# Two small users of PSUM get one bank between them, in quarters, and the other tiles turn through three banks instead of four

## The chip, the cores and the metric

The kernel runs on one core of a Trainium2 chip. The metric is device time in microseconds (us), from one launch. A core has engines that each work through a queue of their own in order: TensorE (PE) for matmuls, VectorE (DVE), ScalarE (ACT), GpSimd (POOL) and SyncE (SP), which here only issues DMAs. PE writes its results into PSUM, which has eight banks of 512 fp32 columns on 128 partitions; DVE and ACT read them there. All data in this kernel are fp32 except masks and an identity.

## The reference

Two blocks stand one after the other, over a residual stream of 2 sequences of 2048 tokens with 128 features. Each block is: modulated layer norm, an attention layer, a gated residual, modulated layer norm, a stack of local attention layers, a gated residual. The first stack has 6 layers with 16 heads and windows of 32 tokens; the second has 2 layers with 8 heads and windows of 64. The change lies in these stacks. One layer of a stack, cut to what matters:

```
def attn_layer(x, Wqkv, qs, ksc, Wo):
    q, k, v = split(x @ Wqkv)                  # heads of 64
    q = l2norm(q) * qs ; k = l2norm(k) * ksc   # a root per token and head
    q, k = rotary(q, k)
    out = local_attention(q, k, v)             # own window and the one before
    return out @ Wo
x = attn_layer(shift_tokens(x)) + x
x = ffn_layer(shift_tokens(x)) + x
```

## The kernel before, in words

`l0_attention` computes the first block's attention (about the first 560 us). `local_models` then does both stacks, and between them the second block's linear attention (`linear`, in pieces called by `lstep`). The stream is held transposed, features on partitions, in `hs[0]` (input of a layer's attention) and `hs[1]` (after its attention).

A layer's attention is done in tiles of 128 tokens. There are 8 layers of 32 tiles, 256 tiles in all, tile number `i`. A loop at the end of `local_models` runs one round per tile, and in a round several tiles are in work at different stages: the projection of tile i+3 (i+4 in the second stack), the transposes and scores of the tiles i+2 and i+1, the mixing and output projection of tile i. The steps that the prediction speaks of, with the PSUM tiles that they use:

- `project` (L862): two matmuls into a wide tile of two banks, `ps_qk` (L871), 16 heads of 64. In the first stack a tile needs two of these, called the first and the second unit here; in the second stack one. ACT squares the wide tile into `sq` (L873). DVE multiplies it by the rotary tables into `r` (L883) and `t` (L888), which POOL adds (L894). The tile `t` has a single buffer. After the last unit, DVE sums the squares of each head (L899, once per unit) and computes the inverse root in eight short instructions on 32 columns (`rsqrt_quick`, L167 to L180; the last one writes `rq_y`). These are called the root chain here. POOL then multiplies `r` by `rq_y` (L906). The sums and three scratch operands of the chain stand in PSUM: they are written into the last unit's `ps_qk`, over the columns already used up.
- `turn` (L925): transposes of `r` (`ps_turn`, L938), copied out by ACT.
- `values` (L945): `ps_v` (L957), copied out by ACT, then moved by DMAs.
- `scores` (L976): a wide tile `ps_s`, with a mask (L988) and 64 small products (L997); DVE takes the maximum (L1005, `mx`) and subtracts it (L1007, `sm`). ACT exponentiates (L1014), DVE sums (L1021) and POOL normalizes (L1023).
- `keys_first_`: transposes `ps_pT` (L1032), copied out by ACT.
- `mix`: 64 small products into `ps_o` (L1050), copied out by ACT (L1056).
- `project_out` (L1059): eight matmuls into 128 columns of a tile `ps_y` (L1067); two DVE instructions add them to `hs` (L1073). Called the output projection here.
- `feed_forward`: after every fourth tile of a sequence, seven pieces (`ps_c`, `ps_r`, `ps_f`, `ps_fy`) that are spread over the following rounds, at most two to a round.

PSUM is given out by two pools. `psA` has two wide buffers (two banks each), which `ps_qk` and `ps_s` take in turn. `psT` has four single banks, which all other tiles, `ps_y` among them, take in turn (`bank(name)`).

The program text gives the instructions in the order of the loop. When the program is built, a scheduler sets the order of each engine's queue in `local_models` and adds the waits; on the chip that order is fixed. Two instructions on different engines that touch the same PSUM tile in one bank, one of them writing, are put one after the other by a wait.

Of the kernel before, what the change touches and what calls it, by code (L numbers as in the profile page):

```python
# [11 lines left out]
F32 = mybir.dt.float32  # L12
# [60 lines left out]
def tile_kernel(ctx: ExitStack, tc: tile.TileContext, a: dict, out: bass.AP):  # L73
    nc = tc.nc
    DRAM = bass.MemoryType.DRAM
    PSUM = bass.MemoryType.PSUM
# [24 lines left out]
    def bc(ap, shape):  # L101
        return ap.to_broadcast(list(shape))
# [59 lines left out]
    def rsqrt_quick(scr, n, pool):  # L162

        x, xm, h, p = scr
        nc.vector.tensor_scalar(xm, x, 1e-24, None, ALU.max)  # L167
        y = pool.tile([128, n], F32, name="rq_g")
        nc.vector.tensor_scalar(
            y.bitcast(I32), xm.bitcast(I32), -0.5, RSQ_SEED, ALU.mult, ALU.add  # L170
        )
        nc.vector.tensor_tensor(p, xm, y, ALU.mult)
        hs_ = pool.tile([128, n], F32, name="rq_h")
        nc.vector.tensor_tensor(hs_, p, y, ALU.mult)
        nc.vector.tensor_tensor(h, p, y, ALU.mult)
        nc.vector.scalar_tensor_tensor(p, h, RSQ_A[0], hs_, ALU.add, ALU.mult)
        for c in RSQ_A[1:3]:
            nc.vector.scalar_tensor_tensor(p, p, c, hs_, ALU.add, ALU.mult)
        r = pool.tile([128, n], F32, name="rq_y", bufs=2)
        nc.vector.scalar_tensor_tensor(r, p, RSQ_A[3], y, ALU.add, ALU.mult)  # L180
        return r
# [526 lines left out]
    def local_models(mA, mB, hs0):  # L708
# [3 lines left out]
        wk = ctx2.enter_context(tc.tile_pool(name="f_k", bufs=1))  # L712
        lw = ctx2.enter_context(tc.tile_pool(name="l_w", bufs=1))
        psA = ctx2.enter_context(tc.tile_pool(name="f_psA", bufs=2, space=PSUM))
        psT = ctx2.enter_context(tc.tile_pool(name="f_psT", bufs=4, space=PSUM))

        def wide(name):

            return psA.tile([128, 1024], F32, tag="A", name=f"ps_{name}")

        def bank(name):
            return psT.tile([128, 512], F32, tag="T", name=f"ps_{name}")


        hs = [hs0, states.tile([128, B, N + 1], F32, tag="hs1", name="hs1")]
# [53 lines left out]
        wts = {}  # L779
# [82 lines left out]
        def project(i, u):  # L862
            g, b, t = tiles[i]
            m, _ = layers[g]
            H, units = m.H, m.units
            tb = tabs[g, t]
            hw = hs[0][:, b, t * 128:(t + 1) * 128]
            pq = wide("qk")
            for j in range(2):
                js = slice(512 * j, 512 * j + 512)  # L870
                nc.tensor.matmul(pq[:, js], lhsT=hw, rhs=wts[g, u][:, js], start=True, stop=True)  # L871
            sq = wk.tile([128, 1024], F32, name="sq", bufs=2)
            nc.scalar.activation(sq, pq, AF.Square)  # L873
            r = wk.tile(
                [128, 1024], F32, tag=f"r{u if len(units) == 2 else i % 2}", name="r", bufs=2
            )
            t2 = wk.tile([128, 1024], F32, name="t2", bufs=1)
            same = units[u][0][0] == units[u][1][0]
            for e in range(1) if same else range(2):
                s = units[u][e][0]  # L880
                hn = 16 if same else 8
                es = slice(512 * e, 512 * e + 64 * hn)
                nc.vector.tensor_tensor(  # L883
                    r[:, es].rearrange("p (h d) -> p h d", d=DH),
                    pq[:, es].rearrange("p (h d) -> p h d", d=DH),
                    bc(tb[:, 0, s].unsqueeze(1), (128, hn, DH)), ALU.mult,
                )
                nc.vector.tensor_tensor(  # L888
                    t2[:, es].rearrange("p (h s d) -> p h s d", s=2, d=32),
                    pq[:, es].rearrange("p (h s d) -> p h s d", s=2, d=32)[:, :, ::-1, :],  # L890
                    bc(tb[:, 1, s].rearrange("p (s d) -> p s d", s=2).unsqueeze(1),
                       (128, hn, 2, 32)), ALU.mult,
                )
            nc.gpsimd.tensor_tensor(r, r, t2, ALU.add)  # L894
            st[i]["r", u], st[i]["sq", u] = r, sq
            if u == len(units) - 1:

                for v in range(len(units)):
                    nc.vector.tensor_reduce(  # L899
                        pq[:, 16 * v:16 * v + 16],  # L900
                        st[i].pop(("sq", v)).rearrange("p (h d) -> p h d", d=DH), AX.X, ALU.add,
                    )
                y = rsqrt_quick([pq[:, k * 32:k * 32 + 2 * H] for k in range(4)], 2 * H, wk)
                for v in range(len(units)):
                    rv = st[i]["r", v].rearrange("p (h d) -> p h d", d=DH)
                    nc.gpsimd.tensor_tensor(  # L906
                        rv, rv, bc(y[:, 16 * v:16 * v + 16].unsqueeze(2), (128, 16, DH)), ALU.mult
                    )
# [150 lines left out]
        def project_out(i):  # L1059
            g, b, t = tiles[i]  # L1060
            m, _ = layers[g]
            NO = m.NO
            oT = st[i].pop("o")
            py = bank("y")
            for c in range(4):
                for s in range(NO):
                    nc.tensor.matmul(  # L1067
                        py[:, 0:128], lhsT=wts[g, "o"][:, c * NO + s, :], rhs=oT[:, s, c, :],
                        start=(c + s == 0), stop=(c == 3 and s == NO - 1),
                    )  # L1070
            for lo, sh in ((0, 0), (64, 1)):
                cs = slice(t * 128 + sh, t * 128 + sh + 128)
                nc.vector.tensor_tensor(  # L1073
                    hs[1][lo:lo + 64, b, cs], py[lo:lo + 64, 0:128], hs[0][lo:lo + 64, b, cs],
                    ALU.add,
                )

# [389 lines left out]
        for i in range(-3, n):  # L1467
# [5 lines left out]
            for j in rounds.get(i, ()):  # L1473
                g, b, t = tiles[j]
                jj = j % per
                nu = len(layers[g][0].units)
                more = g < last
                if g == second and t % 4 == 0:
                    while (b, t // 4) not in ready:
                        lstep()  # L1480
                if nu == 2:
                    project(j, 0)
                if more and jj == 4:
                    load_proj(g + 1, 0)
                if more and jj == 6 and g + 1 == second:
                    models[1].consts()
                if jj == 6 and g == second - 1:
                    linear_consts()
                if more and jj == 8:
                    factors(g + 1)  # L1490
                    if 2 == 2:
                        load_out(g + 1)
                if more and jj == 18:
                    load_ff(g + 1)
                if more and jj == 22:
                    fold_ff(g + 1)
                if nu == 2 and more and jj == per - 1:
                    load_proj(g + 1, 1)
# [6 lines left out]
            for j in rounds.get(i, ()):  # L1505
                g, b, t = tiles[j]
                jj = j % per
                nu = len(layers[g][0].units)
                more = g < last
                project(j, nu - 1)  # L1510
                if nu == 2 and more and jj == per - 1 and g + 1 < second:
                    load_proj(g + 1, 2)
                if nu == 1 and more and jj == per - 1:
                    load_proj(g + 1, 1)
                if b == B - 1 and j + 1 < n:
                    tables(*tiles[j + 1][::2])
# [12 lines left out]
            if i >= 0:  # L1529
                g, b, t = tiles[i]  # L1530
                project_out(i)
                if 2 == 1 and i % per == per - 1 and g < last:
                    load_out(g + 1)
                if t % 4 == 3:
                    feed_forward(g, b, t // 4)
# [9 lines left out]
    with ExitStack() as ctx2:  # L1545
        local_models(m0, m1, hs0)
# [63 lines left out]
```

## Time and profile before

| what | value |
|---|---|
| median of 3 runs | 4936.85 us (4933.53 to 4939.53) |
| the profiled execution's own time | 4928.13 us |
| its span, first to last instruction | 4926.3 us |
| PE busy | 4493.8 us, 91% of the span |
| DVE busy | 3949.1 us, 80% |
| ACT busy | 2637.9 us, 54% |
| POOL busy | 2781.2 us, 56% |
| granted TensorE clock, mean | 0.961 |

Busy means that the engine was executing an instruction; PE's is an upper bound, since matmuls are pipelined. The profile's waits name, for each idle stretch of an engine, the instruction that came after it and the one that ended it. The chain is the work followed back from the last instruction. The profile is of one execution, which took 8.7 us less than the median of the runs.

### The profile page before, as it was taken

The numbers are of one execution on the slowest core, as the hardware profiler recorded it, in microseconds if no ns is written. First come the engines' busy times: TensorE is split into PE (matmuls) and PEld (weight loads), VectorE is DVE, ScalarE is ACT, GpSimd is POOL, SyncE is SP. The second block draws the span as 40 slices with busy tenths as digits, with TensorE's granted clock in tenths as the row PEclk, the third lists the DMA queues.
The fourth block names the chain that finished last, engine by engine and source line by source line (L and its number), as shares of the span: only waits on it lengthen the run. The fifth ranks groups of instructions, "written<-read, shape, count | busy, mean of one in ns | idle before, by whom it ended". The sixth has DMA issues, their size and how long they took to land.

```text
span 4926.3 us, 166334 instructions
## 1 busy us (share of the span) xinstructions
PE 4493.8 (91%) x73028; PEld 3066.5 (62%) x73058; DVE 3949.1 (80%) x6840; ACT 2637.9 (54%) x4207; POOL 2781.2 (56%) x1666
## 2 busy tenths in 40 slices
PE   5667799999999999999999999999999998899997
PEld 4445566666666666666666666666666665556554
DVE  6994488888888888888887888888877777788886
ACT  3223355555555555555555555555555555465554
POOL 3332366666666666666666666666655544455552
PEclk8778899999999999999999999999999999999999
DMA  2000222222222322223222322222212111111121
GB/s 78 1 1 25 85 65 67 69 73 70 69 65 64 87 68 65 66 73 76 68 64 64 79 72 65 66 74 69 68 51 59 50 51 46 37 46 49 51 58 41
DMA packets 222468, 295.31 MB, mean 60 GB/s; under 512 B 75657, under 2 KB 95409, under 8 KB 221745
## 3 DMA queue, kind: packets, MB, share of 16 engines
q1 hardware_dynamic: 221744, 284.67, 22.4%
q8 instruction: 576, 9.44, 0.8%
q14 instruction: 148, 1.20, 0.1%
HBM read 40.98 MB, written 10.75 MB: 10 GB/s over the span
## 4 chain that ended last, share of the span: by engine, by line
PE 49%; DVE 25%; ACT 7%; POOL 5%; issue 3%; DMA 0%; SPq 0%; POOLq 0%; DVEq 0%; ACTq 0%
PE ps_qk L871 12%; PE ps_o L1050 5%; PE ps_v L957 5%; DVE ps_qk L899 5%; PE ps_f L1150 5%; DVE t L888 5%; PE ps_turn L938 4%; PE ps_y L1067 4%; POOL r L894 4%; PE ps_s L997 3%; DVE r L883 3%; PE ps_fy L1175 3%; ACT sq L873 2%; DVE rs L1021 2%; PE ps_pT L1032 2%
## 5 line engine op out<-in xcount | busy, mean ns | idle before, releaser
L894 POOL TENSOR_TENSOR r<-r,t 128x1024 f32<-128x1024 f32 x448 | 1060.2, 2367 | 911.8 <-DVE t L888 794.3
L906 POOL TENSOR_TENSOR r<-r,rq_y 128x1024 f32<-128x1024 f32 x448 | 843.8, 1902 | 517.9 <-DVE rq_y L180 495.8
L873 ACT ACTIVATE sq<-ps_qk 128x1024 f32<-128x1024 f32 x448 | 460.6, 1028 | 1082.3 <-PE ps_qk L871 1014.7
L871 PE MATMUL ps_qk<-wp,hs 128*128 128x512 f32 x1792 | 893.8, 621 | 105.7 <-DVE rq_y L180 77.1
L883 DVE TENSOR_TENSOR r<-ps_qk,tb 128x1024 f32<-128x1024 f32 (+1 forms) x512 | 550.7, 1076 | 211.8 <-ACT sq L873 198.4
L1050 PEld LDWEIGHTS ps_o<-pT,v 64*64 64x64 f32 (+1 forms) x26624 | 479.4, 136 | 304.5 <-ACT pT L1033 160.9
L888 DVE TENSOR_TENSOR t<-ps_qk,tb 128x1024 f32<-128x1024 f32 (+1 forms) x512 | 554.1, 1082 | 143.1 <-POOL r L894 142.4
L1023 POOL TENSOR_TENSOR sm<-sm,rs 128x1024 f32<-128x1024 f32 x256 | 487.5, 1904 | 210.2 <-DVE rs L1022 126.9
L1050 PE MATMUL ps_o<-pT,v 64*64 64x32 f32 (+1 forms) x26624 | 531.2, 221 | 37.0 <-ACT pT L1033 19.2
L899 DVE TENSOR_REDUCE ps_qk<-sq 128x16 f32<-128x1024 f32 x448 | 549.0, 1226 | 11.9
L871 PEld LDWEIGHTS ps_qk<-wp,hs 128*128 128x128 f32 x1792 | 310.1, 193 | 364.3 <-issue 236.1
L938 PEld LDWEIGHTS ps_turn<-ident,r 128*128 128x128 f32 x3584 | 411.7, 143 | 125.2 <-issue 99.4
L957 PE MATMUL ps_v<-wp,hs 128*128 128x512 f32 x896 | 481.9, 639 | 1.0 <-ACT oT L1056 0.8
L1067 PEld LDWEIGHTS ps_y<-oT,wo 128*128 128x128 f32 x3584 | 430.2, 193 | 46.9 <-issue 42.5
L938 PE MATMUL ps_turn<-ident,r 128*128 128x128 f32 x3584 | 447.3, 277 | 9.7 <-POOL r L906 4.1
L1067 PE MATMUL ps_y<-oT,wo 128*128 128x128 f32 x3584 | 446.3, 276 | 1.5 <-ACT oT L1056 1.5
L1056 ACT COPY oT<-ps_o 128x512 f32<-128x512 f32 x448 | 244.0, 588 | 281.9 <-PE ps_o L1050 281.2
L1005 DVE TENSOR_REDUCE mx<-ps_s 128x16 f32<-128x1024 f32 (+1 forms) x256 | 312.5, 1221 | 97.4 <-PE ps_s L997 95.6
L997 PE MATMUL ps_s<-kT,qT 64*32 64x64 f32 (+1 forms) x26624 | 377.9, 230 | 0.7 <-issue 0.5
L997 PEld LDWEIGHTS ps_s<-kT,qT 64*32 64x32 f32 (+1 forms) x26624 | 325.8, 107 | 63.7 <-issue 53.0
L1150 PE MATMUL ps_f<-fx,w 128*128 128x512 f32 (+1 forms) x768 | 356.1, 600 | 2.5 <-DVE fx L1133 1.7
L1021 DVE TENSOR_REDUCE rs<-sm 128x16 f32<-128x1024 f32 (+1 forms) x256 | 310.5, 1213 | 51.1 <-ACT sm L1014 49.0
(265 smaller groups left out, 6850.5 us busy)
## 6 DMA issues: line engine op xcount, KB each, us to landing
v<-vn SPq DMA_DIRECT2D x1276, 128.0 KB
v<-vn SPq DMA_DIRECT2D x744, 64.0 KB
v<-vn SPq DMA_DIRECT2D x64, 256.0 KB
wp<-in_L_ffn_Wqkv SPq DMA_DIRECT2D x20, 512.0 KB
xD<-xb SPq DMA_DIRECT2D x24, 256.0 KB
xb<-xD SPq DMA_DIRECT2D x24, 256.0 KB
cs<-in_cos SPq DMA_DIRECT2D x128, 32.0 KB
cs<-in_sin SPq DMA_DIRECT2D x128, 32.0 KB
```

The lines of the kernel that those rows point to most:

```text
L871: nc.tensor.matmul(pq[:, js], lhsT=hw, rhs=wts[g, u][:, js], start=True, stop=True)
L883: nc.vector.tensor_tensor(r[:, es].rearrange("p (h d) -> p h d", d=DH), pq[:, es].rearrange("p (h d) -> p h d", d=DH), bc(tb[:, 0, s].unsq ...
L888: nc.vector.tensor_tensor(t2[:, es].rearrange("p (h s d) -> p h s d", s=2, d=32), pq[:, es].rearrange("p (h s d) -> p h s d", s=2, d=32)[: ...
L894: nc.gpsimd.tensor_tensor(r, r, t2, ALU.add)
L899: nc.vector.tensor_reduce(pq[:, 16 * v:16 * v + 16], st[i].pop(("sq", v)).rearrange("p (h d) -> p h d", d=DH), AX.X, ALU.add,)
L906: nc.gpsimd.tensor_tensor(rv, rv, bc(y[:, 16 * v:16 * v + 16].unsqueeze(2), (128, 16, DH)), ALU.mult)
L938: nc.tensor.transpose(p[:, c * 128:(c + 1) * 128], r[:, cs], ident)
L957: nc.tensor.matmul(p, lhsT=hw, rhs=wv, start=True, stop=True)
L997: nc.tensor.matmul(sp[W * w:W * w + W, c0:c0 + 2 * W], lhsT=qT[64 * q:64 * q + 64, cc, W * w:W * w + W], rhs=kT[64 * q:64 * q + 64, cc, W ...
L1050: nc.tensor.matmul(po[s][64 * q:64 * q + 64, 128 * c + W * w:128 * c + W * w + W], lhsT=v2[kp, w, co:co + 64], rhs=pT[kp, q, c, W * w:W * ...
L1067: nc.tensor.matmul(py[:, 0:128], lhsT=wts[g, "o"][:, c * NO + s, :], rhs=oT[:, s, c, :], start=(c + s == 0), stop=(c == 3 and s == NO - 1),)
L1150: nc.tensor.matmul(ps_[c][0:sz], lhsT=wts[g, "w1"][:, o:o + sz], rhs=S["x"], start=True, stop=True,)
```

## The change

`psT` gets three banks in place of four. The eighth bank becomes one tile, `ps_quarter`, of four quarters of 128 columns. Quarters 0 and 1 hold the root chain's sums and scratch operands for even and odd tiles, which no longer stand in `ps_qk`. Quarters 2 and 3 take the output projection of even and odd tiles, which no longer takes a bank in turn. The arithmetic is the same, and so are the numbers of instructions.

```diff
-        psT = ctx2.enter_context(tc.tile_pool(name="f_psT", bufs=4, space=PSUM))
+        psT = ctx2.enter_context(tc.tile_pool(name="f_psT", bufs=3, space=PSUM))
+        psQ = ctx2.enter_context(tc.tile_pool(name="f_psQ", bufs=1, space=PSUM))
+        quarters = psQ.tile([128, 4, 128], F32, name="ps_quarter")
+
+        def quarter(kind, i):
+
+            return quarters[:, 2 * kind + i % 2, :]
...
+                ss = quarter(0, i)
                 for v in range(len(units)):
                     nc.vector.tensor_reduce(
-                        pq[:, 16 * v:16 * v + 16],
+                        ss[:, 16 * v:16 * v + 16],
...
-                y = rsqrt_quick([pq[:, k * 32:k * 32 + 2 * H] for k in range(4)], 2 * H, wk)
+                y = rsqrt_quick([ss[:, k * 32:k * 32 + 2 * H] for k in range(4)], 2 * H, wk)
...
-            py = bank("y")
+            py = quarter(1, i)
             for c in range(4):
                 for s in range(NO):
                     nc.tensor.matmul(
-                        py[:, 0:128], lhsT=wts[g, "o"][:, c * NO + s, :], rhs=oT[:, s, c, :],
+                        py, lhsT=wts[g, "o"][:, c * NO + s, :], rhs=oT[:, s, c, :],
...
-                    hs[1][lo:lo + 64, b, cs], py[lo:lo + 64, 0:128], hs[0][lo:lo + 64, b, cs],
+                    hs[1][lo:lo + 64, b, cs], py[lo:lo + 64, :], hs[0][lo:lo + 64, b, cs],
```

## The prediction, made before the changed kernel ran

> **What bounds the kernel now.** I read the page first (shares of the engines, chain), then the windows, PE's waits, and the timeline of one round of the first stack.
>
> ```profile
> PE 4493.8 (91%) x73028; PEld 3066.5 (62%) x73058; DVE 3949.1 (80%) x6840; ACT 2637.9 (54%) x4207; POOL 2781.2 (56%) x1666
> PE 49%; DVE 25%; ACT 7%; POOL 5%; issue 3%; DMA 0%; SPq 0%; POOLq 0%; DVEq 0%; ACTq 0%
> 2000.00:3000.00 1000.00, 966.86 (x18456) 665.36 (x18455) 835.12 (x1350) 572.71 (x900) 642.88 (x375) 0.99 0.28 70
> PE ps_qk L871 <- DVE rq_y L180: 77.1, 79, 3.6
> PE ps_qk L871 <- DVE sm L1007: 16.6, 27, 2.3
> ```
>
> In the window the columns are busy us of PE, PEld, DVE, ACT and POOL, then granted clock, DMA share and GB/s. In the first stack PE is busy 97% of the time and DVE 84%: PE sets the pace with DVE close behind. PE's largest wait in the stacks is the one that the change is about: the first `ps_qk` of a round writes the wide buffer in which the root chain of the round before stood, and waits for the chain's last instruction (77.1 us in 79 waits; with the parts put down to other chain instructions about 88).
>
> One plain round (tile 105, no feed-forward piece on PE), from the timeline; columns are start, duration, instruction, idle time before it and what ended that:
>
> ```profile
> 2356.32 1.98 PE L871 MATMUL ps_qk<-wp,hs 128*128 128x512 f32 x4
> 2358.34 1.03 ACT L873 ACTIVATE sq<-ps_qk 128x1024 f32<-128x1024 f32 x1 [6.68 <-PE ps_qk L871]
> 2359.40 1.22 DVE L883 TENSOR_TENSOR r<-ps_qk,tb 128x1024 f32<-128x1024 f32 x1 [0.49 <-ACT sq L873]
> ...
> 2365.42 1.23 DVE L888 TENSOR_TENSOR t<-ps_qk,tb 128x1024 f32<-128x1024 f32 x1 [1.30 <-POOL r L894]
> ...
> 2366.68 2.49 DVE L899 TENSOR_REDUCE ps_qk<-sq 128x16 f32<-128x1024 f32 x2
> ...
> 2366.93 1.95 PE L1067 MATMUL ps_y<-oT,wo 128*128 128x128 f32 x16
> ...
> 2370.34 0.27 DVE L1073 TENSOR_TENSOR hs<-ps_y,hs 64x128 f32<-64x128 f32 x1
> ...
> 2371.31 0.19 DVE L180 SCALAR_TENSOR_TENSOR rq_y<-ps_qk,rq_g 128x32 f32<-128x32 f32 x1
> ...
> 2371.55 1.98 PE L871 MATMUL ps_qk<-wp,hs 128*128 128x512 f32 x4 [0.75 <-DVE rq_y L180]
> ```
>
> The reader is to see two things. From `r` (2359.40) to the end of the chain (2371.50) DVE has one stretch of 12.10 us with hardly a hole, and `ps_qk` waits only 0.75 us at its end. And the output projection `ps_y` starts at 2366.93, 4.57 us before the chain is over: the two have nothing to do with each other.
>
> **Part 1, what is taken away.** `ps_qk` no longer waits for the chain: at most the 88 us above. The chain's instructions stay the same in number and kind (PSUM before and after), so they cost the same. The first unit's sum (L899, 1.23 us) need not follow the second unit's products any more, but in the order of the built program it still does in most rounds (about seven in ten of those of the first stack), and where DVE has no hole it would gain nothing by moving.
>
> **Part 2, what is added.** Chain and output projection now share a bank. In the order of the changed program as built, the first matmul of an output projection carries a wait for DVE, at the count that the chain's last instruction (L180) raises, in 249 of the 256 rounds; the first `ps_qk` carries none. The output projection is ahead of `ps_qk` in PE's queue, so the wait has moved forward, not gone. Queued behind it on PE are the rest of the scores, both `ps_qk` pairs and the transposes of `ps_pT`; DVE waits for them with `hs`, `mx` and `r`, ACT with `sq`. The scheduler answers by putting part of the scores ahead of `ps_y`: in 84 of the 192 rounds of the first stack 30 or more of the 64 products, in the others none or few (with feed-forward matmuls ahead in most).
>
> The plain round then becomes a loop through both engines. From the chain's end: 0.05 to PE's start (2371.50 to 2371.55), `ps_y` 1.88 (start to the start of the scores, 2366.93 to 2368.81), 15 products left of 64 at 1.48/64 each 0.35, then from `ps_qk` to `r` 3.08 (2356.32 to 2359.40), then DVE's stretch 12.10 less 0.5 for the two `hs` instructions, which now come after `ps_y`: 11.6. Sum 16.96 us against 15.23 before (2356.32 to 2371.55). PE's own work there is 15.23 - 0.75 = 14.5, so PE would stand idle 2.5 us a round. What is late next is the whole of DVE's stretch; DVE in turn idles near 2 us while `ps_y` runs.
>
> The same sum for a group of eight rounds (tiles 104 to 111, which hold two feed-forwards), each time the larger of that loop and of PE's own path between two output projections. Tile 104: PE, 18.85. 105: all scores after `ps_y`, loop 18.3. 106: stretch 13.65 in the trace, loop 18.4. 107: stretch 12.57, loop 17.5. 108: DVE's three `u` (L1167, 0.75 each) go behind the chain in the new order, PE bounds, 19.05. 109: first sum early, 1.2 less, 17.2. 110: 18.0. 111: 16.9. Together 144.2. Before, from one `ps_qk` to the next, the eight took 18.84, 15.23, 16.79, 17.10, 19.58, 17.27, 15.23 and 16.75: 136.8. So +7.4. For tiles 96 to 103 the same working gives 143.0 against 134.3: +8.7. The first stack has 24 such groups: +178 to +209. I take 178, since some rounds (weights being folded) are longer already and give less.
>
> [...] The row: before, `ps_y` ran with the chain from 2366.93 on, in different banks. [...] No run before shows two engines in one bank at once.
>
> **Part 3, three banks.** Without `ps_y` the ring serves fewer tiles, with one bank less. By the timeline each now waits for the copy three uses back: the second `ps_v` for the first `oT`, the transposes for `vn`. These copies take 0.54 to 0.59 us and end before or just at the time when PE comes. Bounds: 0, and one copy of 0.59 in each of 256 rounds, 150 us. Where PE waits at `ps_y` anyway it is covered; I take 0. The feed-forward's `ps_f` takes all three banks, but the transposes behind it now come after `ps_y`, in which time `u` empties them.
>
> **Part 4, second stack** (about 3946 to 4850, 64 rounds of 12.6 to 15.3 us). PE is idle 1.1 us a round there for many reasons, and the chain's waits are about 0.1 of it. One unit, half the output projection, and the new order puts `ps_y` behind other matmuls. Bounds: the old waits vanish, -7; or 1.0 a round as in the first stack, +64. I take +15, nearer the low end, since DVE and PE have more holes there. POOL's and SP's instructions are the same in number; copies of `v` by DMA shift with the rest and end no wait of PE in the rows above. The first 560 us are unchanged.
>
> **Sum.** 178 + 0 + 15 = +193 on the profiled execution's own 4928.13: 5121. The median of the runs lies 8.7 above that execution: 5130.
>
> **Rivals.**
> - *The wait at `ps_y` is short* (20 in 100). In PE-heavy rounds the chain ends 8.0 us after the last `ps_qk` ends (2020.08 to 2028.07 in another part of the timeline), as DVE is then not backed up; PE needs 7.1 us to reach `ps_y` (`ps_o` 2.0, `ps_v` 1.9, `ps_turn` 1.75, part of the scores 1.5). If DVE's stretch closes up like that in plain rounds, 0.9 is lost there in place of 0.75, up to 1.8 where `ps_r` or `fve` lie in it: 2 to 4 us a group, +50 to +95, 4987 to 5030. Against it: the stretch of 12.10 has a single hole of 1.30, which POOL's add sets.
> - *Faster* (8 in 100). The chain is over before PE comes to `ps_y`; 88 us go and nothing comes: 4849. It decides where the loop falls below PE's 14.5, that is when 2.5 of 16.96 go; the sum moved early (1.2) and the `hs` instructions (0.5, already counted) do not reach it.
> - *The three banks bind as well* (12 in 100): ACT squares and exponentiates for 1.03 to 1.06 at a time, and a copy behind that holds PE. Most of Part 3's upper bound added: 5240 to 5280.
>
> My forecast has 60 in 100. The range 4985 to 5215 takes in the first rival, and the second stack's and ring's bounds in part. A difference of 0.2% (10 us) is what a measurement of this kernel tells from none. Faster 0.08, same 0.02, slower 0.90.
>
> **What would show it.** PE's wait list with `ps_quarter` L1074 behind `rq_y` in some 150 to 250 waits of 1 to 3 us, 200 to 350 us in all; `ps_qk` behind `rq_y` gone; PE at 92 to 94% in the middle windows; DVE idle before `hs` for the output projection. If `ps_quarter` waits under 100 us the first rival is right; under 30, the second. Waits of `ps_v` or `ps_turn` for ACT over 50 us would show the third. I am wrong if the plain round is not near 17 us.

## The result, and the profile after

The changed kernel takes 5213.53 us (median of 4 runs, 5207.41 to 5225.7) against 4938.19 for the kernel before on the same chip (4 runs): 1.0566 times, 95% interval 1.0552 to 1.0581. That is 275 us more, where the forecast was 193. The profiled execution took 5225.70 us with a span of 5223.9. By the first `ps_qk` of tiles 0 and 192, the first stack went from 3379.1 to 3684.5 us (+305), the second from 900.6 to 870.2 (-30), and what lies before and after them from 646.6 to 669.2 (+23), although the change does not touch it; in the other runs of the whole kernel it lay between 646 and 666.

From the page of after (busy us of the engines; the chain by engine), then its windows (columns as in the prediction), then its waits, of PE and of DVE (us in total, times, longest):

```profile
PE 4634.7 (89%) x73028; PEld 3128.2 (60%) x73058; DVE 3961.7 (76%) x6840; ACT 2648.3 (51%) x4215; POOL 2778.3 (53%) x1666
PE 41%; DVE 29%; ACT 9%; POOL 6%; issue 4%; DMA 0%; POOLq 0%; DVEq 0%; SPq 0%; ACTq 0%
```

```profile
2000.00:3000.00 1000.00, 921.67 (x16870) 625.43 (x16869) 768.84 (x1237) 525.95 (x825) 584.15 (x338) 0.98 0.25 63
```

```profile
PE ps_quarter L1074 <- DVE rq_y L180: 232.5, 125, 4.0
...
DVE hs L1080 <- PE ps_quarter L1074: 361.2, 188, 5.6
```

The chain's wait is off `ps_qk` and on the output projection, as forecast: 232.5 us in place of 77.1. PE is busy 92% of the middle window instead of 97%. But one number does not fit the forecast's sum. It had PE's own work unchanged, and PE's busy time rose by 140.9 us (4493.8 to 4634.7), nearly as much as its idle time (432.5 to 589.2, +156.7).

The plain round (tile 105), from the timeline of PE and DVE:

```profile
2544.47 1.98 PE L877 MATMUL ps_qk<-wp,hs 128*128 128x512 f32 x4
...
2547.55 1.22 DVE L889 TENSOR_TENSOR r<-ps_qk,tb 128x1024 f32<-128x1024 f32 x1 [0.49 <-ACT sq L879]
...
2558.95 0.19 DVE L180 SCALAR_TENSOR_TENSOR rq_y<-ps_quarter,rq_g 128x32 f32<-128x32 f32 x1
...
2559.19 2.05 PE L1074 MATMUL ps_quarter<-oT,wo 128*128 128x128 f32 x16 [1.20 <-DVE rq_y L180]
...
2561.17 0.45 PE L1004 MATMUL ps_s<-kT,qT 64*32 64x64 f32 x30
...
2561.28 0.59 DVE L1080 TENSOR_TENSOR hs<-ps_quarter,hs 64x128 f32<-64x128 f32 x2 [2.14 <-PE ps_quarter L1074]
...
2561.55 1.98 PE L877 MATMUL ps_qk<-wp,hs 128*128 128x512 f32 x4
```

Read as the loop of the prediction: chain's end, `ps_quarter`, 30 records of the scores, `ps_qk` (2561.55), and from `ps_qk` to `r` 3.08, from `r` to the chain's end 11.59. The round is 17.08 us, where 16.96 was worked out and 15.23 was measured before.

Where the extra time lies is seen round by round, from one `ps_qk` to the next, in us. The last column is the run `c_ring3` below.

| tile | before | forecast | after | ring of three alone |
|---|---|---|---|---|
| 104 | 18.84 | 18.85 | 20.15 | 20.15 |
| 105 | 15.23 | 18.3 | 17.08 | 15.23 |
| 106 | 16.79 | 18.4 | 19.26 | 16.78 |
| 107 | 17.10 | 17.5 | 18.67 | 16.30 |
| 108 | 19.58 | 19.05 | 20.14 | 19.74 |
| 109 | 17.27 | 17.2 | 18.47 | 18.26 |
| 110 | 15.23 | 18.0 | 17.08 | 15.22 |
| 111 | 16.75 | 16.9 | 18.69 | 20.87 |
| sum | 136.8 | 144.2 | 149.5 | 142.6 |

The four rounds that the chain bounds (105, 106, 107, 110) took 72.1 together, and the forecast had 72.2. The four with the long feed-forward pieces `ps_f` and `ps_fy` on PE (104, 108, 109, 111) took 77.5; the forecast had 72.0, about what they had been (72.4). The miss sits there. In 104 and 108 the chain ends 1.28 and 1.96 us before the output projection starts, so PE bounds them. In 109 and 111 the output projection starts 0.05 us after the chain's end, but with at most 0.1 us of idle time before it: there both paths are about equally long.

### The profile page after: what moved, and what is told of

The parts are those of the page before. It is cut to its first block, busy times and chain, and to the rows that moved or that the text cites. A ratio compares the mean times of both kernels' runs of the same rounds, so it can differ in the third digit from the quotient of the medians.

```text
span 5223.9 us, 166290 instructions
## 1 busy us (share of the span) xinstructions
PE 4634.7 (89%) x73028; PEld 3128.2 (60%) x73058; DVE 3961.7 (76%) x6840; ACT 2648.3 (51%) x4215; POOL 2778.3 (53%) x1666
## 4 chain that ended last, share of the span: by engine, by line
PE 41%; DVE 29%; ACT 9%; POOL 6%; issue 4%; DMA 0%; POOLq 0%; DVEq 0%; SPq 0%; ACTq 0%
PE ps_quarter L1074 8%; PE ps_qk L877 8%; DVE t L894 6%; DVE ps_quarter L906 6%; POOL r L900 5%; PE ps_o L1057 4%; PE ps_s L1004 4%; DVE r L889 4%; PE ps_v L964 4%; DVE rs L1028 3%; PE ps_turn L945 3%; PE ps_f L1157 3%; ACT sq L879 3%; PE ps_fy L1182 2%; ACT sm L1021 2%
## 5 line engine op out<-in xcount | busy, mean ns | idle before, releaser
L1074 PE MATMUL ps_quarter<-oT,wo 128*128 128x128 f32 x3584 | 505.3, 297 | 234.5 <-DVE rq_y L180 232.5
L1074 PEld LDWEIGHTS ps_quarter<-oT,wo 128*128 128x128 f32 x3584 | 466.4, 207 | 303.7 <-DVE rq_y L180 266.8
L1057 PEld LDWEIGHTS ps_o<-pT,v 64*64 64x64 f32 (+1 forms) x26624 | 501.6, 136 | 244.7 <-ACT pT L1040 169.2
L1057 PE MATMUL ps_o<-pT,v 64*64 64x32 f32 (+1 forms) x26624 | 550.1, 222 | 49.6 <-issue 23.7
L906 DVE TENSOR_REDUCE ps_quarter<-sq 128x16 f32<-128x1024 f32 x448 | 545.8, 1218 | 5.3 <-ACT sq L879 0.4
L945 PE MATMUL ps_turn<-ident,r 128*128 128x128 f32 x3584 | 462.7, 277 | 13.2 <-POOL r L913 7.5
L964 PE MATMUL ps_v<-wp,hs 128*128 128x512 f32 x896 | 468.2, 640 | 2.3 <-ACT oT L1063 1.6
L1080 DVE TENSOR_TENSOR hs<-ps_quarter,hs 64x128 f32<-64x128 f32 x512 | 147.9, 289 | 365.9 <-PE ps_quarter L1074 361.2
L1004 PE MATMUL ps_s<-kT,qT 64*32 64x64 f32 (+1 forms) x26624 | 396.2, 233 | 8.6 <-issue 5.2
```

Source lines behind the costliest of these rows:

```text
L906: nc.vector.tensor_reduce(ss[:, 16 * v:16 * v + 16], st[i].pop(("sq", v)).rearrange("p (h d) -> p h d", d=DH), AX.X, ALU.add,)
L945: nc.tensor.transpose(p[:, c * 128:(c + 1) * 128], r[:, cs], ident)
L964: nc.tensor.matmul(p, lhsT=hw, rhs=wv, start=True, stop=True)
L1004: nc.tensor.matmul(sp[W * w:W * w + W, c0:c0 + 2 * W], lhsT=qT[64 * q:64 * q + 64, cc, W * w:W * w + W], rhs=kT[64 * q:64 * q + 64, cc, W ...
L1057: nc.tensor.matmul(po[s][64 * q:64 * q + 64, 128 * c + W * w:128 * c + W * w + W], lhsT=v2[kp, w, co:co + 64], rhs=pT[kp, q, c, W * w:W * ...
L1074: nc.tensor.matmul(py, lhsT=wts[g, "o"][:, c * NO + s, :], rhs=oT[:, s, c, :], start=(c + s == 0), stop=(c == 3 and s == NO - 1),)
```

## Experiments

### The parts alone

Three kernels, each with one half of the change or less. `c_ring3` is the kernel before with a ring of three and the eighth bank unused; the other two are the changed kernel with one of the two users of the eighth bank put back:

```diff
c_ring3 (against before)
-        psT = ... tc.tile_pool(name="f_psT", bufs=4, space=PSUM)
+        psT = ... tc.tile_pool(name="f_psT", bufs=3, space=PSUM)
a_root_alone (against after)
-            py = quarter(1, i)
+            py = bank("y")[:, 0:128]
b_out_alone (against after)
-                ss = quarter(0, i)
+                ss = pq
```

> The kernel before with three banks in the ring and the eighth bank unused. Theory: the missing bank costs little, 4935 to 4985 us. Rival (the missing bank is a large part): 5050 us or more.

> The eighth bank holds the root chain alone; the output projection goes back into the ring, which keeps three banks. Theory (the loss is the order that the shared bank forces: output projection behind the chain): no matmul waits for the chain any more, so the time is at or below the kernel before, 4840 to 4945 us. Rival (three banks in the ring are a large part of the 275 us): 5000 us or more, with waits of ps_v, ps_turn or ps_f for ACT copies in PE's list.

> The eighth bank holds the output projections alone; the root chain stands in ps_qk again, the ring has three banks. Theory: ps_qk waits for the chain as before (about 80 to 100 us in PE's list), ps_quarter does not; 4920 to 4970 us. Rival (three banks, or the output projection in a bank of its own that DVE must empty each round): 5000 us or more.

Against 4939.4 for the kernel before, measured beside them: `c_ring3` 5025.09 (1.0176, 1.0159 to 1.0194), `a_root_alone` 4950.08 (1.002, 1.0001 to 1.0038), `b_out_alone` 5006.61 (1.0144, 1.0125 to 1.0163). So the ring of three alone costs 86 us; next to it, taking the chain out of `ps_qk` brings 75 and taking the output projections out of the ring brings 18. Only when both users are in the one bank does the time go to 5213: moving the output projection alone out of the chain's bank (`a_root_alone` against after, one line) is worth 263 us, although the ring then has more to serve. None of the three met its range: `c_ring3` lies between its theory and its rival, `a_root_alone` 5 us above its theory, and `b_out_alone` where its rival was, all on the dear side.

What the ring costs is seen in the weight loads' list of waits, of before and of `c_ring3`:

```profile
PEld ps_v L957 <- ACT oT L1056: 3.1, 10, 1.1
```

```profile
PEld ps_v L957 <- ACT oT L1056: 82.8, 181, 0.9
...
PEld ps_pT L1032 <- ACT pT L1033: 23.2, 26, 1.1
```

The first is the wait that Part 3 named, the copy three uses back, at 0.46 us each; the changed kernel has it too (`ps_v` behind `oT`, 82.4 us in 183). The second Part 3 did not name. Both stand in the list of the loads; in that of the matmuls they come to 1.3 and 1.2 us, while PE's busy time is 66 us longer than before (4559.9 against 4493.8). Part of the timeline of tile 104, one line of the kernel before, then `c_ring3`:

```profile
2344.57 2.07 PE L1050 MATMUL ps_o<-pT,v 64*64 64x32 f32 x128
```

```profile
2404.45 0.60 PE L1032 MATMUL ps_pT<-ident,sm 128*128 128x128 f32 x4
...
2404.89 1.02 PE L871 MATMUL ps_qk<-wp,hs 128*128 128x512 f32 x2
...
2406.00 0.66 PE L1032 MATMUL ps_pT<-ident,sm 128*128 128x128 f32 x4
...
2407.44 2.90 PE L1050 MATMUL ps_o<-pT,v 64*64 64x32 f32 x128
```

Before, `ps_pT` was one group of eight, and `ps_o` took 2.07 (2344.57 to 2346.64). With three banks the second half starts only as the copy of the first ends (2405.95), while the second and third tile of `ps_f` are read from 2406.99 on; the queue has half a projection in between, and `ps_o` takes 2.90. This round is 18.84 us with four banks (before, `f_half`) and 20.15 in after, `a_root_alone`, `b_out_alone`, `c_ring3`, `g_split`, `g_half` and `e_short`, the kernels with three that keep the place of the output projection. The 20.87 of tile 111 in `c_ring3` is another thing: PE stands idle for 1.50 us inside `ps_o`, for nothing that the profile shows, and the `ps_v` behind it takes 3.42 us (1.98 before) at a granted clock of 0.57. With the same ring this round is 17.53 in `a_root_alone`.

### The chain behind the output projection

`d_chain_behind` keeps the shared bank and issues the chain after the round's output projection instead of ahead of it:

```diff
                 project_out(i)
+            for j in rounds.get(i, ()):
+                root(j)          # the sums, the chain and POOL's multiply, taken out of project
```

> The changed kernel with the shared bank, but the root chain of a round is given after that round's output projection, so the order in the bank is turned round: the chain waits for the projection, and the projection only for the chain of the round before, long done. Theory: the loss is in the order, so most of the 275 us come back, 4870 to 5000 us, with waits of ps_quarter for rq_y under 40 us. Rival (a bank shared by PE and DVE is slow in itself, or the ring): 5130 us or more.

It took 5841.65 us (1.1833, 1.1815 to 1.1851), far above the theory; the rival's "5130 or more" takes it in, but for a cause that it did not name. The wait at `ps_quarter` is gone, but now the chain ends late, and the transposes behind it wait for POOL's multiply:

```profile
PE ps_turn L948 <- POOL r L916: 367.1, 240, 4.4
```

So this run does not tell what sharing costs; it shows that a later chain costs far more than a later output projection.

### Sharing taken away in another way, and a shorter chain

`g_split` is the changed kernel with the root's operands in SBUF; `e_short` the changed kernel with a shorter chain.

```diff
g_split
-                ss = quarter(0, i)
+                ss = wk.tile([128, 128], F32, tag="cg", name="ss")
e_short
-                    tensor_reduce(ss[:, 16 * v:16 * v + 16], sq[v] by heads)
+                    w = len(units) - 1 - v
+                    if v == 0: tensor_reduce(ss[:, 16 * w:16 * w + 16], sq[w] by heads)
+                    else: tensor_copy(ss[:, 16 * w:16 * w + 16], sq[w], first column of each head)
```

> The changed kernel with one thing taken back: the root's operands stand in a small tile of SBUF, so that the eighth bank holds the projected outputs alone; the ring of three banks and the quarters for the outputs stay. If the wait on the shared bank (and the slow matmuls after it) is what costs, the three single effects add up: 4939 + 86 (ring of three, measured alone) - 75 (root out of the projections' buffer) - 18 (outputs out of the ring) = about 4931, 4900 to 4965; ps_quarter behind rq_y is gone, and the projections of the output (L1074) take about 354 us of PE in the first stack instead of 411. The rival, that the three banks and the changed order of issue make most of the loss and the wait only shows it, expects more than 5050.

> The changed kernel with a shorter chain: in the first stack one unit's sum of squares (L906, 1.25 us) is replaced by a copy of 16 columns; the sum of that unit is left out of the root. The chain is about 1.05 us shorter in 192 rounds. By the loop alone (chain's end, output projection, projections, r, chain) each round that the chain bounds, 5 to 8 of 8, gives 1.05: 130 to 200 us less than 5213, so 5013 to 5080, and the output projection keeps its 411 us of PE in the first stack. If a slower TensorE clock after the idle time is the second part of the loss, shorter idle time also makes those matmuls faster: L1074 falls below 385 us in the first stack, another 30 to 58 us, 4955 to 5050. If the chain did not bound the round, less than 60 us would come.

`g_split` took 5051.71 us (1.0253, 1.0231 to 1.0275): 162 less than after, but 121 more than the 4931 of the sum, and by its time alone in the rival's range. By the trace it is not the rival: the wait for the chain is gone from PE's list, the output projections take 451.1 us of PE (505.3 in after), and the first stack is 3446.5 us, 238 less than in after and below the 3460.8 of `c_ring3`. What was not expected is in the groups by form: the chain's first instruction, from and to SBUF (the first line, of `g_split`), against the same from and to PSUM (the second, of `a_root_alone`); after the count come busy us and the mean ns of one:

```profile
L167 DVE TENSOR_SCALAR ss<-ss 128x32 f32<-128x32 f32 x192 | 149.8, 780 | 5.3
```

```profile
L167 DVE TENSOR_SCALAR ps_quarter<-ps_quarter 128x32 f32<-128x32 f32 x192 | 38.0, 198 | 5.2
```

DVE's busy time is 156 us above after's (4118.2 against 3961.7), and the second stack takes 952.9 us instead of 870.2. Taking the scratch out of PSUM has a price, then (the last section shows what goes with it), and this run understates what the shared bank costs.

`e_short` took 5174.59 us (1.05, 1.0474 to 1.0526): 39 less, where 130 or more were expected (67 less by the profiled executions, all of it in the first stack). By the text put on record, under 60 means that the chain does not bound the round; the timeline says otherwise. The chain did get shorter. Its plain round, tile 105:

```profile
2504.94 1.22 DVE L889 TENSOR_TENSOR r<-ps_qk,tb 128x1024 f32<-128x1024 f32 x1 [0.49 <-ACT sq L879]
...
2514.26 0.74 PE L1006 MATMUL ps_s<-kT,qT 64*32 64x64 f32 x50
...
2515.29 0.19 DVE L180 SCALAR_TENSOR_TENSOR rq_y<-ps_quarter,rq_g 128x32 f32<-128x32 f32 x1
...
2515.54 2.05 PE L1076 MATMUL ps_quarter<-oT,wo 128*128 128x128 f32 x16 [0.54 <-DVE rq_y L180]
...
2517.52 1.02 PE L1006 MATMUL ps_s<-kT,qT 64*32 64x64 f32 x78
```

From `r` to the chain's end it is 10.54 us instead of 11.59. But the order was made anew when the program was built, and 78 records of the scores now stand behind the output projection instead of 30: 0.58 us more on the same loop. The round fell by 0.47 (17.08 to 16.61), not by 1.05. Nor did the output projections get faster, which was the second hope: 504.8 us of PE against 505.3, although their waits are shorter (190.8 us in 115). The run supports the loop, since what lies between the chain's end and `ps_qk` counts in full, and it shows that an edit to one instruction is also an edit to every queue.

### The clock

The page's group of the output projection, of before and of after, in 3584 records each:

```profile
L1067 PE MATMUL ps_y<-oT,wo 128*128 128x128 f32 x3584 | 446.3, 276 | 1.5 <-ACT oT L1056 1.5
```

```profile
L1074 PE MATMUL ps_quarter<-oT,wo 128*128 128x128 f32 x3584 | 505.3, 297 | 234.5 <-DVE rq_y L180 232.5
```

The same matmuls take 59 us more. In the rounds of tiles 106, 107 and 110 the timeline reads as in the first fence. The second has the windows of two such stretches, of the rounds of tiles 105 and 106 (the third number from the end is the granted clock):

```profile
2576.73 3.53 PE L1074 MATMUL ps_quarter<-oT,wo 128*128 128x128 f32 x16 [2.51 <-DVE rq_y L180]
...
2595.99 2.96 PE L1074 MATMUL ps_quarter<-oT,wo 128*128 128x128 f32 x16 [2.44 <-DVE rq_y L180]
...
2652.82 2.05 PE L1074 MATMUL ps_quarter<-oT,wo 128*128 128x128 f32 x16 [2.42 <-DVE rq_y L180]
```

```profile
2559.20:2561.20 2.00, 2.00 (x21) 1.88 (x22) 0.00 (x0) 0.00 (x0) 1.92 (x2) 1.00 0.71 172
2576.70:2580.20 3.50, 3.47 (x18) 3.35 (x18) 0.00 (x0) 0.00 (x0) 3.38 (x2) 0.55 0.17 40
```

After 1.20 us of idle time the group took 2.05 at a clock of 1.00, after 2.51 us it took 3.53 at 0.55. In tile 110 it took 2.05 again after 2.42, so such a wait does not always do it. To measure that by itself, `m_gap` and `m_gap2` run this loop and nothing of the reference:

```diff
+    for n in (0, 256, 512, 768, 1024, 1536, 2048, 3072):      # columns, 32 times each
+        24 matmuls 128x512 into pw ; copy pw to w
+        if n: two tensor_scalar, n and 128 columns, into w     # the wait
+        16 matmuls 128x128 from w ; copy out
```

> No part of the reference is computed: TensorE runs 24 matmuls of 128x512, then waits for VectorE for a set time (eight lengths, 32 times each, about 0.5 to 6 us), then runs 16 matmuls of 128x128 as the output projection does. By the theory of a clock that falls after idle time, the 16 take about 2 us after waits under 1.5 us, 2 or up to 3.6 us after waits of 2 to 3 us, and 3.4 us or more after waits over 4 us, with the granted clock near 0.55 in those stretches. By the rival, that the slow ones in the changed kernel come from the operands or the bank, the 16 take the same time after every wait.

> No part of the reference is computed. As the run m_gap, with every matmul in one PSUM tile, so that TensorE really waits: 24 matmuls of 128x512, a wait for VectorE of one of eight lengths, 16 matmuls of 128x128, 32 times each. If the clock falls after idle time, the 16 take about 2 us after short waits, a mixture after waits of 2 to 3 us, and 3.4 us or more after the longest, with the granted clock near 0.55 in those stretches. If slow bursts in the changed kernel come from operands or bank, they take the same time after every wait.

`m_gap` told nothing: its two PSUM tiles let TensorE run the next 24 matmuls during the wait, and it was busy 100% of the span of 6220.6 us, at a granted clock of 0.999. In `m_gap2`, with one tile, the waits before the 16 matmuls were 0.78 to 2.96 us, and the 16 matmuls, two records each, took 3.56 us or about 5 from the first start to the last. The slow ones: none of 160 after waits of 0.78 to 1.90, 3 of 32 after 2.16, 2 of 32 after 2.43, 18 of 32 after 2.96. Two with the same wait, from its timeline and its windows (here only PE's busy time, then the clock):

```profile
432.65 5.46 PE L1562 MATMUL ps_one<-w,ident 128*128 128x128 f32 x32 [2.96 <-DVE w L1560]
...
650.09 3.84 PE L1562 MATMUL ps_one<-w,ident 128*128 128x128 f32 x32 [2.96 <-DVE w L1560]
```

```profile
432.65:437.80 5.15, 5.15 (x31) 0.67 0.00 0
650.09:653.60 3.51, 3.51 (x31) 1.00 0.00 0
```

The operands and the bank are the same after every wait, so in this loop it is the idle time that goes with the slow matmuls, and after 0.78 to 1.90 us it did not happen. In the stacks it did: in `e_short`, 16 of the 45 output projections behind waits of 1.77 to 1.88 us took 2.46 us or more. One of them, and its window (here only PE, then the clock):

```profile
680.83 3.54 PE L1076 MATMUL ps_quarter<-oT,wo 128*128 128x128 f32 x16 [1.83 <-DVE rq_y L180]
680.80:684.35 3.55, 3.52 (x24) 0.55 0.51 131
```

So cutting many of the waits from 2.4 to 1.8 us did not bring these matmuls back to speed: what the slow groups of the first stack took over 2.05 us each is 44 us in both kernels. In the loop 24 matmuls of 128x512 stand ahead of the wait, in the stacks the scores and transposes; whether that makes the difference was not tried. After the same 2.96 us 18 of 32 were slow and 14 were not, so the length of the wait alone does not decide; what else does is not shown.

### The place of the output projection

`j_late` is the changed kernel with one thing moved: the output projection of a tile is issued a round later, behind the next first pair of `ps_qk`. `k_late_before` makes the same move in the kernel before.

```diff
             if i >= 0:
-                project_out(i) ; feed_forward(...) after every fourth tile
...
                 project(j, 0)
+                project_out(i - 1) ; feed_forward(...) after every fourth tile
```

> The changed kernel (shared bank, ring of three, chain all in PSUM) with the output projection of a tile issued one round later, behind the next first pair of ps_qk; nothing is left out. By the theory that the loss comes from where the projection stands in PE's queue when the chain ends, the wait for rq_y at ps_quarter nearly goes (under 40 us), L1074 falls from 411 to about 355 us of PE in the first stack, and the time is 5213 less 230 of idle time less 56 and a little more for the columns that follow: 4900 to 4990. If one bank for both costs in itself, the wait stays over 100 us and the time is over 5080.

> The kernel before (root in the projections' buffer, ring of four) with the output projection of a tile issued one round later, behind the next first pair of ps_qk; nothing is left out. If the later place is good only where ps_qk does not wait for the chain, then PE has nothing left to do while the chain ends: in plain rounds the output projection (1.9 us) no longer lies beside the chain's end, the wait at ps_qk grows from 77 us to 200 to 400, and the time is 5040 to 5250. If the later place is a gain by itself, as in j_late, it is 4870 to 4920 and the wait stays under 100.

`j_late` took 4911.01 us (0.9942, 0.9921 to 0.9963), 302 less than after and less than the kernel before. The bank is shared as before, the ring has three banks, the chain is the same. From its list of waits and its groups by form:

```profile
PE ps_quarter L1074 <- DVE rq_y L180: 10.4, 19, 1.2
```

```profile
L1074 PE MATMUL ps_quarter<-oT,wo 128*128 128x128 f32 x3584 | 451.0, 278 | 11.4 <-DVE rq_y L180 10.4 <-ACT oT L1063 0.3 <-issue 0.3
```

The slow matmuls went with the wait (505.3 to 451.0 us). So one bank for both costs little at this place; what cost most was the projection's place between the chain's end and the next `ps_qk`.

`k_late_before` took 4940.09 (1.0024, 1.0011 to 1.0037; 4929.08 for the kernel before, beside it): no gain by the place alone, and my 5040 to 5250 was wrong too. I had added the output projection to the time that PE stands idle at `ps_qk`. In its round of tile 110 the `ps_qk` wait did grow (1.70 us, round 15.72 against 15.23), but the loop from `ps_qk` through DVE to the chain's end does not hold the output projection in either order; the wait for the chain is 92.5 us in 85, against 77.1. The move pays only with the chain out of `ps_qk`: 0.9942 against 1.0024.

### Versions that beat both

`f_half` is the kernel before with the chain's last two operands in SBUF, so that `ps_qk` is free after L172, and no `tensor_scalar` works from SBUF to SBUF. `g_half` has the same next to a ring of three and the output projections in the eighth bank. `k_late_half` is `f_half` with the later output projection. With all four operands in SBUF (`f_sbuf`) the kernel before does not fit into SBUF (28.28 KB a partition for its pool, 27.31 left), so there is no time for it. (By the listing `rsqrt_quick` has nine instructions, not eight, since L178 stands for two; L172 is the third.)

```diff
-                y = rsqrt_quick([pq[:, k * 32:...] for k in range(4)], 2 * H, wk)
+                ps_ = wk.tile([128, 128], F32, tag="cg", name="rq_s")
+                y = rsqrt_quick([pq[:, k * 32:...] for k in range(2)]
+                                + [ps_[:, k * 32:...] for k in range(2)], 2 * H, wk)
```

> The kernel before with one edit: the last two of the root's four operands in SBUF, the first two where they were, so that ps_qk is free after the fourth of the chain's ten instructions, 1.3 us earlier; ring of four, output projections in the ring. Of the 77 to 88 us of waits at ps_qk 50 to 80 go: 4855 to 4890. If the wait only moves to another matmul, or the SBUF operands slow the chain, 4920 to 4960.

> Ring of three, output projections alone in the eighth bank (as in the run b_out_alone), and the root's first two operands in the projections' buffer as before, its other two in SBUF, so that no tensor_scalar works from SBUF to SBUF and ps_qk is free seven chain instructions (1.3 us) earlier. No bank is shared between the chain and the output projection. If the single effects add up (4939 + 86 for the ring, -18 for the outputs, -50 to -75 for the wait at ps_qk) it is 4925 to 4960, and the chain's instructions stay at 0.19 to 0.21 us each. If the ring of three and the new order cost more next to a free chain than alone, it is over 5000.

> As k_late_before, with the last two of the root's operands in SBUF as in the run f_half, so that ps_qk waits for the fourth of the chain's ten instructions, 1.3 us before its end. If the place of the output projection is bad where ps_qk waits for any part of the chain, 4960 to 5150; if the two gains (41 in f_half, 29 in j_late) add, 4860 to 4890.

`f_half` took 4899.29 us (0.9919, 0.9902 to 0.9935): 41 of the 50 to 80 hoped for. `ps_qk` behind `rq_y` is gone, but 16.6 us in 16 waits stand behind L172, and 41.1 us in 53 waits are now put down to `sm` (16.6 in 27 before). `g_half` took 4985.41 (1.0084, 1.0059 to 1.011), above its range. It is 86 us slower than `f_half` on the same chip, for the ring of three and the bank of the output projections together; with the chain in `ps_qk` the same two cost 67 (`b_out_alone` against before). `k_late_half` took 4864.39 (0.9875, 0.9854 to 0.9897), the fastest of all: the two moves together gave 65 us.

## Why the prediction was right or wrong

**What bounds, Part 1 and Part 2.** Right. The wait left `ps_qk` and came back larger at the output projection, which is the likeliest case and not the first or second rival. The plain round is 17.08 for 16.96. The forecast's new idle time in the first stack was 266 less 88, +178; by the starts in the trace PE's idle time there rose by 173 (315.4 against 142.6). The waits are fewer than the 150 to 250 foretold (125), at 232.5 us within the 200 to 350. Single rounds were further off than their sum: 105 and 110 came out 1.2 and 0.9 shorter, and 106 and 107 came out 0.9 and 1.2 longer, with the slow matmuls in them; that these cancelled was luck. For 105 the working had all scores behind the output projection; in the trace 98 of their 128 records are ahead of it, in 110 too, and DVE's stretch is the 11.6 of the plain round in both.

**Part 3, the ring taken at 0: the term that failed.** The working had the waits right (the second `ps_v` for the first `oT`, 0 to 150 us) and chose the wrong end: measured alone it is 86. The reason given, that PE waits at `ps_y` anyway and so covers it, holds in the rounds that the chain bounds. It does not hold in the rounds with feed-forward matmuls, where PE has no wait to hide it in: in `c_ring3` the rounds 105, 106 and 110 are unchanged (15.23, 16.78, 15.22) and 104, 108, 109 and 111 are longer. In after these four grew by 5.0 us together (72.4 to 77.5), and the forecast had them shrink by 0.4. The reason given for `ps_f`, that the transposes come when `u` has emptied its banks, failed for the `ps_pT` right behind it (tile 104). With 86 in that term the sum would have been 279, 4 us from the 275 of the medians, but by luck: in the profiled executions it would have had 264 in the first stack for 305, 15 in the second for -30, and nothing in the rest for 23. The third rival, 5240 to 5280 on this mechanism, had too much of it, though its sign came: `ps_v` waits for ACT 82.4 us in the list of the loads, over the 50 named. How much of the 275 is the ring's inside the changed kernel is not shown: no run has four ring banks next to the shared bank. That it was 20.15 us for tile 104 in after and in `c_ring3` alike is the nearest to it.

**PE's own work unchanged: the assumption that failed.** Busy time rose by 140.9. Of it 59 is the output projection: 44 lie in the 43 of 187 unbroken groups of the first stack that took over 2.4 us instead of 2.05, and 39 of these stand behind a wait of over 1.5 us. `c_ring3`, where no group took so long, has 11 more than before in these matmuls and 66 more in all (4559.9). The sum had no term for a wait that slows the matmuls behind it.

**Part 4.** Wrong in sign: the second stack fell by 30 us where 15 more were forecast. `a_root_alone` has 882.5 and `j_late` 878.5 there, `c_ring3` 901.0, so most of it comes with the chain leaving `ps_qk`. I had put the chain's waits there at 0.1 us a round.

**One bank for both.** The wait was there (232.5 us in 125), so the quarters were one resource in this kernel as built, and the 88 us of the second rival did not come off. Whether two engines could have worked in one bank at once was not tried.

## What to carry to other kernels

When two users are put into one PSUM bank, draw the loop from the end of one to whatever the pacing engine does next: a matmul that must wait for a chain belongs behind the work that starts the next chain, not ahead of it, and here that place alone was worth 302 us. Price a smaller ring by the rounds in which the engine that uses it has no other wait, because there it is not covered (20.15 us for 18.84 in tile 104, and 15.23 as before in tile 105). And scratch freed a few instructions earlier can do what a bank of its own does: two operands moved to SBUF (0.9919) beat the whole change, and with the later place they gave 0.9875.

## What the hardware showed that I had not expected

TensorE's granted clock was lower behind some of the idle times: 0.67 behind 2.96 us in the loop, 0.55 behind 2.51 us in the changed kernel and behind 1.83 us in `e_short`. In the loop none of 160 groups was slow after up to 1.90 us and 18 of 32 after 2.96; in `e_short` it was 16 of 45 after 1.77 to 1.88. In the changed kernel a group of 16 records that takes 2.05 took 3.53 after 2.51 us of waiting, so that wait cost 4.0 us (2.51 + 3.53 - 2.05).

A `tensor_scalar` of 32 columns took 780 ns on average from SBUF to SBUF (`g_split`) and 198 ns from PSUM to PSUM (`a_root_alone`), in the same place of the chain. In the trace of `g_split` 195 of the 256 instructions of L167 in the stacks took over 0.3 us; each of these began while an instruction of POOL ran, and ended 0.03 to 0.05 us after it. The other 61 found POOL idle or within 0.27 us of its end. One of the 195, and the instruction of POOL that it outlasts (1511.96 against 1511.92):

```profile
1509.57 2.35 POOL L900 TENSOR_TENSOR r<-r,t 128x1024 f32<-128x1024 f32 x1
...
1511.30 0.66 DVE L167 TENSOR_SCALAR ss<-ss 128x32 f32<-128x32 f32 x1
```

From and to PSUM, in after, 232 of the 256 began while POOL ran, and none took over 0.20 us.
